# Row maxima of attention scores: from a PE transpose to a round trip through DRAM

## The chip, the cores and the metric

The kernel runs on one core of a Trainium2 chip. The metric is the device time of one execution in microseconds (us); lower is better. A core has five engines that run side by side, each working through its own instructions in order: PE (TensorE, matrix products; PEld are its weight loads), DVE (VectorE), ACT (ScalarE), POOL (GpSimd) and SP (SyncE), which here does nothing but issue DMA transfers. Engines wait for each other, and for transfers, through semaphores.

## The reference

The input x has 4 batches of 1024 tokens with 128 features. The block is half a mixture-of-experts FFN, attention, and half the same FFN again, each on a layer norm of x and added to x. The attention, cut to what matters here, with 16 heads of 64:

```python
scores = jnp.einsum('bhqd,bhkd->bhqk', q, k) * scale
attn = jax.nn.softmax(scores, axis=-1)
out = jnp.einsum('bhqk,bhkd->bhqd', attn, v)
out = out.transpose(0, 2, 1, 3).reshape(b, s, H * DH)
out = out @ w_out.T + residual
```

The softmax needs the largest score of each query row. The kernel computes it before the scores that it exponentiates.

## The kernel before

The three stages are FFN, attention and FFN. Attention takes most of the time, and the change lies in it.

**Units and slots.** Attention is cut into 64 units `U`: two heads (`hh` 0 and 1) of one batch by 512 queries. A unit has 8 slots, one for each 128 keys; two slots are a group `g`, so a unit is 4 groups. The loop over `g` (L908) writes each engine's instructions in the order in which Python emits them; nothing reorders them later. `self.at(g, fn)` puts `fn` into a list for the end of group `g`, and `run_later(g)` (L930) runs that list in the order of entry. So `at(self.group, ...)` means the end of the group being emitted, and `at(self.group + 1, ...)` the end of the next.

**Two passes.** `passA` runs 15 slots ahead (`AHEAD`). It computes a rough score tile of 128 queries by 512 keys for both heads into the PSUM tile `ps_a` (L675), and DVE reduces it to maxima (L676). After the eighth part of a unit, L679 folds the two halves of keys and negates: `m8` is 128 partitions (query within a block) by 8 columns (2 heads by 4 query blocks), and `max_row` is scheduled.

`score` computes the transposed scores, keys on partitions and queries along the free dimension, as four products added in PSUM (L703). The fourth multiplies a row of ones with `maxr[U % 2]`, whose rows 0 and 64 hold the negated maxima of the two heads for the unit's 512 queries; that subtracts each query's maximum. `maxr` therefore needs each maximum in a row, while `m8` has it in a column. ACT exponentiates (L707), `values` multiplies with the latents (L726).

**How the maxima become rows.** `max_row` transposes `m8` on PE against an identity into one of two spare banks of `ps_s` (L685), DVE copies the 8 x 128 result to `mr` (L687), and one group later two DMAs, one for each head, write 4 x 128 floats each into row 0 or 64 of `maxr` (L689).

**Denominators.** `den(U)` (L730) sums the exponentials on PE, ACT copies them to `dsb`, and then the sums make a trip through DRAM: `d<-dsb` and `dT<-d` (L745, L746) at the end of the next group, a reciprocal on DVE (L754), `d<-rT` and two `rB<-d` broadcasts (L757, L759) at the end of the group after that. DVE multiplies with `rB` two groups later (L766), and the output products (L771) follow. `dT<-d` reads what `d<-dsb` wrote, so SP waits for that transfer to land before it issues the next, and all that SP has behind it waits too.

**SP's list.** All DMAs are issued by SP, in order: loads of Q and K for the unit pair three ahead (`QT<-qs`, `KT<-ks`, four at a time), rotary-embedding results to DRAM (`qs` or `ks` `<-hi_r` and `<-eo`), latents fetched (`C_l<-cs`), the denominators' trip, and the maxima. Completion is counted on eight semaphores used in turn, so a DMA also waits for the one eight places before it where that is not known to be over.

Of the kernel before, what the change touches and what calls it, by code (L numbers as in the profile page):

```python
# [9 lines left out]
F32 = mybir.dt.float32  # L10
F32R = mybir.dt.float32r
# [26 lines left out]
class Kernel:  # L38
# [625 lines left out]
    def passA(self, a):  # L664

        nc = self.nc
        U, i = divmod(a, 8)
        P, half = divmod(U, 2)
        qb, kk = divmod(i, 2)
        if i == 0:  # L670
            self.m_of[U] = self.ms.tile([128, 2, 4, 2], F32, name="m")
        q0 = half * 512 + qb * 128
        for hh in range(2):
            r = slice(64 * hh, 64 * hh + 64)
            nc.tensor.matmul(self.psA[:, hh, :], self.QT[P % 3][r, 0, q0:q0 + 128], self.KT[P % 3][r, 0, kk * 512:kk * 512 + 512], start=True, stop=True)  # L675
        nc.vector.tensor_reduce(self.m_of[U][:, :, qb, kk], self.psA, AX.X, ALU.max)  # L676
        if i == 7:
            m = self.ms.tile([128, 8], F32R, name="m8")
            nc.vector.tensor_reduce(m, self.m_of.pop(U).rearrange("p h q k -> p (h q) k"), AX.X, ALU.max, negate=True)  # L679
            self.at(self.group + 1, lambda: self.max_row(U, m))  # L680

    def max_row(self, U, m):
        nc = self.nc
        pt = self.aux()
        nc.tensor.transpose(pt[0:8, 0:128], self.f(m), self.ident)  # L685
        mr = self.ms.tile([8, 128], F32R, name="mr")
        nc.vector.tensor_copy(mr, pt[0:8, 0:128])  # L687
        for hh in range(2):
            self.at(self.group + 1, lambda hh=hh: self.dma(out=self.maxr[U % 2][64 * hh:64 * hh + 1, :], in_=mr[4 * hh:4 * hh + 4, :]))  # L689

    def score(self, s, hh, k):

# [335 lines left out]
```

## Time and profile before

| What | Value |
|---|---|
| Median of 3 runs | 1803.73 us (1801.5 to 1804.94) |
| The profiled execution | 1803.11 us, of which its span is 1801.3 us |
| Busy: PE / PEld / DVE / ACT / POOL | 1726.3 / 1030.3 / 1339.9 / 908.9 / 1339.3 us |
| First FFN stage (0 to 260 us), PE busy | 218.7 us |
| Attention (260 to 1650 us), PE busy | 1372.5 us |
| Last FFN stage (1650 to 1801 us), PE busy | 135.2 us |
| Transposes L685 | 64, 0.27 us each |
| Copies to `mr`, L687 on DVE | 64, 0.27 us each |
| DMAs `maxr<-mr` | 128, 0.63 us of SP each, 2 KB each |
| From their issue to landing (semaphore events), median | 1.9 us |
| DMAs `dT<-d` / `d<-rT` (128 rows of 32 B) | 1.6 / 1.4 us from issue to landing, median |

The span runs from the first to the last instruction of the core. A row of the timeline gives the start in us from the beginning of the span, the length in us, engine, line of the kernel, operation, output and inputs by name, their shapes, and how many instructions were merged into the row; a bracket at its end gives the idle time before it and the instruction that ended that. An SP row is the time for issuing a DMA only; when its data has landed is seen in the semaphore events, and the bytes moved in the packet records.

### The profile page before, as it was taken

Reading aid. Unit: us, or ns where it says so; the run is one execution under the profiler, and the core shown is the slowest. Engines: PE = TensorE matmul, PEld = TensorE weight load, DVE = VectorE, ACT = ScalarE, POOL = GpSimd, SP = SyncE. Lnnn points to the kernel's source line nnn. Section 1 sums busy time; section 2 is a strip of 40 time slices with the busy share of each in tenths; the row PEclk is TensorE's granted clock in tenths of the full one; section 3 lists DMA queues with packets and bytes.
Section 4 is the critical chain, followed back from the end, with each engine's and each line's share of the span. In section 5 each row is a group of like instructions: output and inputs, shape, how many; then the busy total and the mean of one; then the engine's idle time right before and its main releaser. Section 6 shows DMA issues by size and latency. Waiting matters only on the chain.

```text
span 1801.3 us, 31304 instructions
## 1 busy us (share of the span) xinstructions
PE 1726.3 (96%) x11492; PEld 1030.3 (57%) x11492; DVE 1339.9 (74%) x1903; ACT 908.9 (50%) x1916; POOL 1339.3 (74%) x803
## 2 busy tenths in 40 slices
PE   7988889999999999999999999999999999999898
PEld 5777655555555555555555555555555555556676
DVE  6776658877777778777688777788777776835787
ACT  4666555444545445554444445454444444445454
POOL 4458678778887788877788777788888765556566
PEclk9999989999999999999999999999999999999899
DMA  6025445444444444454444544454444432124443
GB/s 196 1 71 170 135 129 165 145 145 147 130 142 142 150 145 130 130 153 142 141 135 136 160 140 131 143 142 147 136 144 140 130 95 72 31 96 129 129 124 100
DMA packets 129674, 232.80 MB, mean 129 GB/s; under 512 B 36336, under 2 KB 49776, under 8 KB 128880
## 3 DMA queue, kind: packets, MB, share of 16 engines
q1 hardware_dynamic: 129520, 230.80, 42.7%
q8 instruction: 90, 1.47, 0.4%
q14 instruction: 64, 0.52, 0.1%
HBM read 146.45 MB, written 84.02 MB: 128 GB/s over the span
## 4 chain that ended last, share of the span: by engine, by line
PE 78%; DVE 7%; ACT 7%; POOL 3%; issue 3%; DMA 1%; SPq 1%; ACTq 0%; POOLq 0%; DVEq 0%
PE psc L726 24%; PE ps_s L703 21%; PE ps_a L675 8%; PE ps_s L738 5%; ACT p L707 4%; PE psx L771 4%; PE ps_s L400 3%; PE ps_s L479 3%; PE psx L593 2%; DVE m L676 2%; PE psc L371 1%; PE psc L479 1%; PE psx L434 1%; PE ps_s L434 1%; ACT dtmp L383 1%
## 5 line engine op out<-in xcount | busy, mean ns | idle before, releaser
L676 DVE TENSOR_REDUCE m<-ps_a 128x2 f32<-128x1024 f32 x512 | 627.3, 1225 | 324.1 <-PE ps_a L675 323.9
L707 ACT ACTIVATE p<-ps_s 128x512 f32<-128x512 f32 x1024 | 531.0, 601 | 605.6 <-PE ps_s L703 605.4
L719 POOL TENSOR_TENSOR acc<-acc,p 128x1024 f32<-128x1024 f32 x256 | 609.7, 2382 | 43.0 <-ACT p L707 31.6
L726 PE MATMUL psc<-p,ckn 128*64 128x512 f32 x2048 | 496.2, 605 | 0.0
L703 PE MATMUL ps_s<-QT,KT 64*128 64x512 f32 x3072 | 447.3, 393 | 0.1
L719 POOL TENSOR_TENSOR acc<-p 128x1024 f32<-128x1024 f32 x64 | 152.2, 2377 | 251.4 <-ACT p L707 251.3
L703 PEld LDWEIGHTS ps_s<-QT,KT 64*128 64x128 f32 x3072 | 296.7, 185 | 60.2 <-issue 3.2
L726 PEld LDWEIGHTS psc<-p,ckn 128*64 128x64 f32 x2048 | 124.3, 136 | 213.7 <-issue 199.4
L675 PE MATMUL ps_a<-KT,QT 64*128 64x512 f32 x1024 | 234.6, 450 | 11.2 <-DVE m L676 11.0
L675 PEld LDWEIGHTS ps_a<-KT,QT 64*128 64x128 f32 x1024 | 98.5, 184 | 229.9 <-issue 83.8
L703 PE MATMUL ps_s<-maxr,one_row 64*128 64x512 f32 x1024 | 210.0, 392 | 1.0 <-DMA maxr<-mr 1.0
L612 POOL TENSOR_TENSOR eo<-eo,hi_r 128x512 fp32r<-128x512 f32 x128 | 185.0, 1463 | 0.0
L766 DVE TENSOR_TENSOR osb<-osb,rB 128x512 f32<-128x512 f32 x64 | 153.8, 2403 | 3.0 <-DMA rB<-d 3.0
L384 POOL TENSOR_TENSOR X<-X,dtmp 128x512 f32<-128x512 f32 x54 | 69.0, 1278 | 73.2 <-ACT dtmp L383 66.7
L703 PEld LDWEIGHTS ps_s<-maxr,one_row 64*128 64x128 f32 x1024 | 103.4, 185 | 23.0 <-DMA maxr<-mr 2.2
L487 POOL TENSOR_TENSOR p<-eo,p 128x512 fp32r<-128x512 f32 x42 | 62.6, 1496 | 42.0 <-ACT p L486 35.5
L602 POOL TENSOR_TENSOR eo<-rt,rt 128x512 f32<-128x512 f32 x64 | 81.8, 1279 | 0.0
L600 POOL TENSOR_TENSOR eo<-rt,rt 128x512 f32<-128x512 f32 x64 | 81.8, 1278 | 0.0
L607 ACT CAST hi_r<-eo 128x512 fp32r<-128x512 f32 x128 | 74.6, 640 | 6.9 <-DMA qs<-hi_r 3.6
L400 PE MATMUL ps_s<-xs,wg 128*128 128x512 f32 x192 | 66.6, 457 | 11.8 <-DVE p L408 10.7
L728 ACT COPY osb<-psc 128x512 f32<-128x512 f32 x64 | 37.6, 588 | 72.8 <-PE psc L726 72.8
L771 PEld LDWEIGHTS psx<-G,osb 128*128 128x128 f32 x496 | 60.8, 193 | 21.2 <-issue 21.2
(194 smaller groups left out, 2131.8 us busy)
## 6 DMA issues: line engine op xcount, KB each, us to landing
C_l<-cs SPq DMA_DIRECT2D x64, 512.0 KB
QT<-qs SPq DMA_DIRECT2D x256, 128.0 KB
KT<-ks SPq DMA_DIRECT2D x256, 128.0 KB
qs<-hi_r SPq DMA_DIRECT2D x32, 512.0 KB
qs<-eo SPq DMA_DIRECT2D x32, 512.0 KB
ks<-hi_r SPq DMA_DIRECT2D x32, 512.0 KB
ks<-eo SPq DMA_DIRECT2D x32, 512.0 KB
rB<-d SPq DMA_DIRECT2D x128, 128.0 KB
```

Source lines behind the costliest of these rows:

```text
L400: nc.tensor.matmul(p, w[:, a, e, :], xs[:, c, :], start=k == 0, stop=k == 2)
L600: nc.gpsimd.tensor_tensor(w["eo"][:, 0, :], w[0, 0], w[1, 1], ALU.subtract)
L612: nc.gpsimd.tensor_tensor(eo.bitcast(F32R), eo, self.f(w["hi"][:, int(stage[2]), :]), ALU.subtract)
L675: nc.tensor.matmul(self.psA[:, hh, :], self.QT[P % 3][r, 0, q0:q0 + 128], self.KT[P % 3][r, 0, kk * 512:kk * 512 + 512], start=True, stop= ...
L676: nc.vector.tensor_reduce(self.m_of[U][:, :, qb, kk], self.psA, AX.X, ALU.max)
L703: nc.tensor.matmul(ps, w, x, start=k == 0, stop=k == 3)
L707: nc.scalar.activation(self.p_of[s][:, hh, :], ps, AF.Exp, scale=0.125)
L719: nc.gpsimd.tensor_tensor(acc, self.p_of[s - 1] if c == 1 else acc, self.p_of[s], ALU.add)
L726: nc.tensor.matmul(self.psC[64 * hh:64 * hh + 64, :], self.ckn[b % 2][:, c, :], self.p_of[s][:, hh, :], start=c == 0, stop=c == 7)
L738: nc.tensor.matmul(pd[32 * n:32 * n + 32, 0:256], self.ones, part[:, n // 2, 256 * (n % 2):256 * (n % 2) + 256], start=k == 0, stop=k == D ...
L766: nc.vector.tensor_tensor(osb, osb, rB, ALU.mult)
L771: nc.tensor.matmul(po[:, i * 128:(i + 1) * 128], osb[:, i * 128:(i + 1) * 128], self.G[:, j, :], start=True, stop=True)
```

## The change

The transpose, the copy to `mr` and the two DMAs go. At the end of the group in which L679 runs (one group earlier than the transpose was) a DMA writes `m8` as it is to a DRAM tile `d3` of 128 x 8. At the end of the next group (one group earlier than the old DMAs) a single DMA fills rows 0 and 64 of `maxr` from there. Its source walks `d3` along columns: for each head `h` and query block `q` the 128 values `p`, which lie 8 floats apart. There are four such DRAM tiles, used in turn. The values that reach `maxr` are the same as before.

```diff
@@ -677,16 +677,13 @@
         if i == 7:
             m = self.ms.tile([128, 8], F32R, name="m8")
             nc.vector.tensor_reduce(m, self.m_of.pop(U).rearrange("p h q k -> p (h q) k"), AX.X, ALU.max, negate=True)
-            self.at(self.group + 1, lambda: self.max_row(U, m))
+            self.at(self.group, lambda: self.max_row(U, m))
 
     def max_row(self, U, m):
         nc = self.nc
-        pt = self.aux()
-        nc.tensor.transpose(pt[0:8, 0:128], self.f(m), self.ident)
-        mr = self.ms.tile([8, 128], F32R, name="mr")
-        nc.vector.tensor_copy(mr, pt[0:8, 0:128])
-        for hh in range(2):
-            self.at(self.group + 1, lambda hh=hh: self.dma(out=self.maxr[U % 2][64 * hh:64 * hh + 1, :], in_=mr[4 * hh:4 * hh + 4, :]))
+        d = self.dram.tile([128, 8], F32, name=f"d3_{U % 4}")
+        self.dma(out=d, in_=m)
+        self.at(self.group + 1, lambda: self.dma(out=self.maxr[U % 2][0:128:64, :].rearrange("h (q p) -> h q p", p=128), in_=d.rearrange("p (h q) -> h q p", h=2)))
```

## The prediction

> **What bounds the kernel now.** I read the stretches of the span first, then the chain of waits. The row below is the attention stage: length, then the busy time of PE, PEld, DVE, ACT and POOL.
>
> ```profile
> 260.00:1650.00 1390.00, 1372.46 (x9683) 750.00 (x9681) 1043.28 (x1306) 684.97 (x1373) 1087.43 (x584) 1.00 0.44 132
> ```
>
> ```profile
> PE 78%; DVE 7%; ACT 7%; POOL 3%; issue 3%; DMA 1%; SPq 1%; ACTq 0%; POOLq 0%; DVEq 0%
> ```
>
> PE is busy for 1372 of 1390 us at full clock (1.00), and 78% of the chain that ended last is PE. An instruction taken off PE here shortens the span by nearly its own pace; DMA matters only where its landing comes after the moment at which an engine of that chain wants the data. DVE (1043 us) has room on average, but works in order.
>
> Then I read the timeline of one cycle. A unit U (8 slots, 4 groups) takes 21 to 23 us; this is the end of one group and the next two.
>
> ```profile
> 910.00 2.25 SPq L47 DMA_DIRECT2D KT<-ks  x4
> ...
> 912.35 0.52 SPq L745 DMA_DIRECT2D d<-dsb  x1
> ...
> 913.78 0.39 PE L593 MATMUL psx<-C_l,wup 64*128 64x512 f32 x1
> 913.78 0.39 PE L593 MATMUL ps_s<-C_l,wup 64*128 64x512 f32 x1
> ...
> 914.11 0.27 PE L685 MATMUL ps_s<-ident,m 128*8 128x128 f32 x1
> ...
> 914.31 1.94 PE L726 MATMUL psc<-p,ckn 128*64 128x512 f32 x8
> ...
> 915.31 0.33 SPq L746 DMA_DIRECT2D dT<-d  x1
> ...
> 916.17 2.28 SPq L47 DMA_DIRECT2D QT<-qs  x4
> ...
> 920.55 0.20 DVE L754 RECIPROCAL rT<-dT 128x8 f32<-128x8 f32 x1
> ...
> 920.77 0.34 SPq L757 DMA_DIRECT2D d<-rT  x1
> 921.11 1.23 DVE L676 TENSOR_REDUCE m<-ps_a 128x2 f32<-128x1024 f32 x1 [0.37 <-PE ps_a L675]
> ...
> 922.37 1.15 SPq L759 DMA_DIRECT2D rB<-d  x2
> 922.76 0.40 PE L675 MATMUL ps_a<-KT,QT 64*128 64x512 f32 x2
> ...
> 923.61 1.35 SPq L47 DMA_DIRECT2D maxr<-mr  x2
> ```
>
> The transpose (L685) sits in PE's stream between the rope products and the values. The two maxr DMAs go out at 923.61, at the tail of SP's list, where nothing urgent follows. The denominators' round trip through DRAM (d<-dsb, dT<-d, reciprocal, d<-rT, rB<-d) runs through the middle of SP's list, and DVE's reciprocal stands in front of a reduce on which PE's next passA waits.
>
> **What goes: PE and DVE.** In the 55 cycles with rope products ahead, the first L726 matmul starts 0.13 us after the preceding matmul's end; without a transpose between, L726 starts 0.07 us before it (193 cases after den, outp and others). So a transpose costs 0.20 us of PE's pace: 55 x 0.20 = 11.2 us, and 8 late cycles (0.26 to 0.51 us gaps) give 3.0 more: 14 us. I count 0.85 of it, since the stage's PE is not on the chain in every cycle (DVE and ACT hold 14%): **12 us**. DVE loses 64 casts of 0.27 us, 17 us. DVE's reduces wait 324 us for PE in all, so I count nothing. PSUM bank ps_s is released earlier; its next writer comes after PE's 1.94 us of values anyway.
>
> **What goes: waits for maxr.** PE, weight loads included, waited 3.2 us for the old DMA. The new gather is issued near 912.3 in place of 923.6 for a use at 926.8 (the first maxr product of the unit), so these waits go. I count 1 us, as some of them stand behind a late reciprocal.
>
> **What is added on SP.** The old pair of DMAs takes 2 x 0.63 us of issuing per unit. The new write of the column block (128 rows of 32 B, like d<-rT: 0.33 us to issue, 1.4 us to land) needs the L679 reduce (906.79) and is issued near 907.0, when SP stands idle until 909.58 (ks<-hi_r). Nothing is delayed by it. The gather (nearest row d<-dsb, 0.52 us; few rows per DMA) takes its place a group later, after KT<-ks and **ahead of d<-dsb and dT<-d**: the listing of SP's instructions has KT x4, gather, d<-dsb, dT<-d, ks<-eo, QT x4, d<-rT. Its own wait, for the column block, is over some 4 us earlier. Behind it stand the denominators.
>
> **What the gather costs.** It moves 1024 single floats: 4 KB, 4 B each. The trace of before has no such DMA. Its semaphore events show that a DMA with 128 rows posts 16 of them and one with 4 rows (d<-dsb, maxr<-mr) only 5. The Trainium skill ("DMA: Bandwidth & Descriptors", in "Why a DMA increments its semaphore by 16 and not by 1") says that the engine count is the largest up to 16 that divides the outermost dimension of both sides, and, under "Rules for kernel authors", that a strided last dimension becomes one descriptor per element. Both speak against this change: outermost is 2, so 512 descriptors fall on each of 2 engines. Spread as the 128-row rows are, it would be 64 each.
>
> The price of a descriptor from the packet records: in lnsb<-in_ln_sb (128 pieces of 8 B from DRAM) the eight packets of one engine start 5.9 ns apart, and so do the 32 B packets of dT<-d. A packet of 4 to 32 B is recorded as 7 to 9 ns long. With 256 B (wv, 1024 packets) starts of one engine are about 14 ns apart. So 512 descriptors take 3.0 us at 5.9 ns, 4.6 us at 9 ns, 7.2 us at 14 ns. A floor is the 16-engine reading: 64 x 5.9 ns = 0.4 us. Generating 1024 descriptor pairs is not slower: those 1024 packets all started within 1.6 us. I take **3.0 us**, the pace of the rows nearest in size, though those bursts are 8 long and not 512. The same page's fit of a DMA's time ("Anatomy of one DMA": 2.0 us plus bytes over 436 GB/s, for another issuing path) would make it 2.0 us like any 4 KB transfer, delaying nothing; it has no term for descriptors, so the packet rows decide.
>
> **What is late next.** d<-dsb has 4 rows, so by the same rule it uses engines that the gather fills. The median KT transfer takes 4.1 us to land, so both queue behind KT, and d<-dsb lands later by about the gather's 3.0 us. SP waits for that before dT<-d: 915.3 becomes 918.4. The cover is the time from the landing of dT to the reciprocal. By the semaphore events it is about 3.7 us in the units where KT loads precede (every second one, 32), and 5.3 to 6.5 us in the others. PE's gain takes 0.2 us of it. After it come 0.37 us in which DVE was idle before L676, and 0.42 us between the end of that reduce (922.34) and the passA at 922.76. So a gather costs nothing up to 3.5 + 0.8 = **4.3 us**, or 8.4 ns a descriptor, in one half, and up to about 6.8 us in the other; each us beyond is paid by PE, 32 times per half. At 3.0 us the cover holds. A few units have less (2.3 to 3.1 us before the 0.8): 1 us in all. The held-up ks<-eo and QT loads issue 3 us later and then push d<-rT by 0.7 us; the time from rB's landing to its use is 4.5 us at the median, and QT pieces are used some five groups later. The gather lands near 918, used at 926.8: covered up to about 12 us.
>
> **Sum.** 1803.1 (profiled execution: span 1801.3 and 1.8 around it; 0.6 below the median of 1803.7) - 12 - 1 + 1 = **1791 us**.
>
> **Rivals.**
> - *Descriptors at 9 to 14 ns* (for: their recorded length, 9 ns; 512 in a row may not sustain a burst's pace; against: measured starts at 5.9). At 12 ns the gather is 6.1 us: 1.8 us past the cover in 32 units, +58 us against -12: **1849 us**. This is the case on the other side: the reciprocal waits for dT, DVE's reduce stands behind it, PE stands for passA. It decides from 9.1 ns (4.65 us), where 32 x 0.37 us eat the 12.
> - *Descriptors bound by latency*, over 14 ns (for: no long run of tiny reads is in the trace; against: 256 B packets already flow at 14). At 7.2 us: 2.9 x 32 + 0.4 x 32 = 106, so **1897 us**; at 23 ns (11.8 us) both halves pay, 240 + 160, near 2190.
> - *The transpose's time was not on the path* (for: DVE's and ACT's 14% of the chain; against: PE at 98.7% of this stage): gather hidden, PE's gain lost in waits on the exponentials, **1803 us**.
>
> **How the numbers follow.** Forecast 48%, its own range 1786 to 1798 (all 14 us and the 3 us of waits gained; or half the gain and cover missing in some units). Slower descriptors 27%, latency-bound 20%, no effect 5%. A change within 0.2% (3.6 us) can't be told from none. Faster by more: nearly all of the forecast, 47%; within: the no-effect case and 9 ns, 9%; slower 44%. The range runs from 1786 to 1895 and leaves out the latency case.
>
> **What would show it.** Right: L726 follows L593 at -0.07 us; the gather shows as 1024 packets of 4 B over about 3 us; dT<-d issues 3 us later after d<-dsb; DVE's reciprocal shows no wait for dT. Wrong: a row in which the reciprocal waits for dT<-d in half or all of the units, and PE's passA then waits for DVE's m; or a wait for maxr on PE.

## The result, and the profile after

The changed kernel takes a median of 1787.79 us (1782.91 to 1791.76, 6 runs) against 1804.54 us (1801.5 to 1805.81, 6 runs) for the kernel before: a ratio of 0.9905, 95% interval 0.9887 to 0.9923, or 14 to 20 us less. The forecast was 1791 us. Run again at the end of the study (run r1) it took 1781.15 us against 1806.01, ratio 0.9868 (0.9853 to 0.9884), 21 to 27 us less, which is below the forecast's own range of 1786 to 1798 us. The sign is certain; by the ratios the size differs by 7 us between two sessions of the same two kernels, and a good part of that goes with the granted clock (see "What stays open").

The first view is the attention stage by windows, columns as in the prediction (length, busy time of PE, PEld, DVE, ACT, POOL, granted clock, share and rate of the DMA engines), of the kernel after.

```profile
260.00:1650.00 1390.00, 1374.49 (x9697) 752.95 (x9694) 1041.16 (x1261) 691.43 (x1386) 1095.34 (x589) 1.00 0.48 134
```

Next the chain of waits on the page of the kernel after.

```profile
PE 78%; DVE 7%; ACT 7%; DMA 2%; POOL 2%; issue 2%; SPq 1%; ACTq 0%; DVEq 0%; POOLq 0%
```

PE still bounds the stage: busy for 1374 of 1390 us, 78% of the chain. A bound that has not moved gives back what was taken off it. Only DMA has grown, from 1% to 2%, and the busy share of the DMA engines from 0.44 to 0.48.

Where the time went is seen when the execution is cut at the starts of four matmuls: the first of all, the first and the last product with `maxr`, and the last of all.

| Profiled execution | From the first matmul to the first product with `maxr` | To the last product with `maxr` | To the last matmul |
|---|---|---|---|
| before | 237.5 us | 1386.8 us | 166.6 us |
| after | 242.3 us | 1372.2 us | 165.6 us |
| after, run r1 | 236.1 us | 1365.7 us | 165.6 us |

The gain is in attention, 14.6 and 21.1 us. In the first profile of the changed kernel 4.8 us were lost in the first FFN stage, at a mean granted clock of 0.93 in 0 to 260 us against 0.96 in the profile before; in r1 (0.96) they are not there. So that loss is not the change's.

The timeline of the cycle that the prediction read, in the kernel after (start in us, length in us, engine, line, operation):

```profile
910.47 2.27 SPq L47 DMA_DIRECT2D KT<-ks  x4
...
912.85 0.56 SPq L47 DMA_DIRECT2D maxr<-d  x1
...
913.51 3.89 SPq L742 DMA_DIRECT2D d<-dsb  x1
...
914.25 0.39 PE L593 MATMUL ps_s<-C_l,wup 64*128 64x512 f32 x1
...
914.58 1.94 PE L723 MATMUL psc<-p,ckn 128*64 128x512 f32 x8
...
919.03 0.34 SPq L743 DMA_DIRECT2D dT<-d  x1
...
920.81 0.19 DVE L751 RECIPROCAL rT<-dT 128x8 f32<-128x8 f32 x1
...
921.37 1.23 DVE L676 TENSOR_REDUCE m<-ps_a 128x2 f32<-128x1024 f32 x1 [0.36 <-PE ps_a L675]
```

Between the last rope product (ends at 914.64) and the first product of the values (914.58) nothing stands any more: the values start 0.06 us before the other's end, where they started 0.13 us after it. On SP the gather goes out between KT and `d<-dsb`, as listed. `dT<-d` follows `d<-dsb` 5.52 us after the latter's start, where before it took 2.96 (912.35 to 915.31). The reciprocal starts 1.78 us after `dT<-d` was issued, against 5.24 before: of the cover that hid the gather, hardly anything is left.

The tile view of the DRAM tiles `d` in the kernel after (count, then minimum, median and maximum of SP's time for issuing one, in ns) shows something that the prediction did not have.

```profile
L47 SPq DMA_DIRECT2D d<-m x64: 320/338/783, 215.3 to 1588.8; - x64
...
L742 SPq DMA_DIRECT2D d<-dsb x64: 523/3465/4338, 279.5 to 1626.2; - x64
```

Issuing `d<-dsb`, right behind the gather, holds SP for 3.47 us, where it was 0.52 before. So SP itself stands while the gather's descriptors drain, and not only the data of `d<-dsb` come later. The column write `d<-m` is cheap to issue, as predicted (0.34 us). The waits of SP's queue in the kernel after (total us, times, longest) show that it is not cheap to wait for:

```profile
SPq L47 <- DMA d<-m: 82.5, 33, 8.3
```

That is every second unit, and the timeline of SP shows why:

```profile
883.44 0.61 SPq L47 DMA_DIRECT2D C_l<-cs  x1
884.09 2.26 SPq L47 DMA_DIRECT2D KT<-ks  x4
886.45 0.37 SPq L47 DMA_DIRECT2D d<-m  x1
889.42 0.38 SPq L47 DMA_DIRECT2D qs<-hi_r  x1
893.70 0.56 SPq L47 DMA_DIRECT2D maxr<-d  x1
894.36 3.45 SPq L742 DMA_DIRECT2D d<-dsb  x1
```

There the column write is issued behind a load of latents and four KT loads, 1 MB in all. By the semaphore events it lands 4.3 us or more after its issue in three quarters of these units (at most 7.2), and the gather goes out 0.1 us after that.

What is left of the cover is read from the waits of the kernel after. These are the reciprocal's waits for `dT<-d`, first of the kernel before, then of the kernel after:

```profile
DVE rT L754 <- DMA dT<-d: 10.7, 2, 6.6
...
DVE rT L751 <- DMA dT<-d: 23.1, 12, 15.1
```

One place, near the end of attention, makes 15.1 of the 23.1 us; the other eleven make 8.0 us. No wait for `maxr` is left on PE.

Of the waits of PE and its weight loads before, the longest that names something which the change removes is that of passA's weight loads for DVE's copy (first line: us in all, times, longest). After, they wait nearly as long for a rope instruction of DVE (second line):

```profile
PEld ps_a L675 <- DVE mr L687: 47.1, 58, 0.8
...
PEld ps_a L675 <- DVE rt L581: 40.6, 50, 0.8
```

What such a wait is worth is tested by e1b, which brings the copy back. The page's line on DMA packets of the kernel after shows the gathers by their number; before, 36,336 packets were under 512 B.

```profile
DMA packets 203528, 233.05 MB, mean 130 GB/s; under 512 B 110704, under 2 KB 123632, under 8 KB 202736
```

64 gathers of 1024 floats are 65,536 of the 74,368 that were added, and 64 column writes of 128 rows another 8,192.

### The profile page after: what moved, and what is told of

It is laid out like the page before. It is cut to its first block, busy times and chain, and to the rows that moved or that the text cites. A ratio compares the mean times of both kernels' runs of the same rounds, so it can differ in the third digit from the quotient of the medians.

```text
span 1790.0 us, 30996 instructions
## 1 busy us (share of the span) xinstructions
PE 1716.9 (96%) x11428; PEld 1025.4 (57%) x11428; DVE 1323.8 (74%) x1839; ACT 907.5 (51%) x1916; POOL 1338.6 (75%) x803
## 4 chain that ended last, share of the span: by engine, by line
PE 78%; DVE 7%; ACT 7%; DMA 2%; POOL 2%; issue 2%; SPq 1%; ACTq 0%; DVEq 0%; POOLq 0%
PE psc L723 25%; PE ps_s L700 21%; PE ps_a L675 8%; PE ps_s L735 5%; ACT p L704 4%; PE psx L768 4%; PE ps_s L400 3%; PE ps_s L479 3%; PE psx L593 2%; DVE m L676 2%; PE psc L371 1%; DMA d<-dsb 1%; PE psc L479 1%; PE psx L434 1%; PE ps_s L434 1%
## 5 line engine op out<-in xcount | busy, mean ns | idle before, releaser
L675 PE MATMUL ps_a<-KT,QT 64*128 64x512 f32 x1024 | 234.1, 451 | 9.5 <-DVE m L676 9.2
L675 PEld LDWEIGHTS ps_a<-KT,QT 64*128 64x128 f32 x1024 | 97.2, 184 | 230.9 <-issue 86.2
L700 PE MATMUL ps_s<-maxr,one_row 64*128 64x512 f32 x1024 | 206.4, 391 | 0.0
L700 PEld LDWEIGHTS ps_s<-maxr,one_row 64*128 64x128 f32 x1024 | 100.2, 184 | 21.1
L735 PE MATMUL ps_s<-p,ones 128*32 128x256 f32 x1024 | 68.5, 385 | 4.7 <-ACT p L704 0.9
```

Of the source, the lines that this page charges most:

```text
L700: nc.tensor.matmul(ps, w, x, start=k == 0, stop=k == 3)
L735: nc.tensor.matmul(pd[32 * n:32 * n + 32, 0:256], self.ones, part[:, n // 2, 256 * (n % 2):256 * (n % 2) + 256], start=k == 0, stop=k == D ...
```

## The experiments

Three theories stood at the start. **The prediction's:** the transposes' pace on PE is the gain, all else is covered. **Order:** the maxima only come earlier, and the gain is from waits for `maxr`. **Collision:** the gather costs a good part in front of the denominators, so that a better place would give more. Kernels of one session share runs of the kernel before: e1, e1b, e2b and e3 (1802.99 us); e4, e5 and e6 (1805.72); e3c, e9 and e10 (1801.9); r1 and r2 (1806.01). Ratios are against those.

**e1 and e1b: the transposes back, the new DMAs kept.** The transpose stands where it was and nothing reads it; e1b also has DVE's copy.

The edit of e1, in `max_row` behind the gather:

```diff
+        def dead():
+            nc.tensor.transpose(self.aux()[0:8, 0:128], self.f(m), self.ident)
+
+        self.at(self.group + 1, dead)
```

And what e1b has beyond it:

```diff
         def dead():
-            nc.tensor.transpose(self.aux()[0:8, 0:128], self.f(m), self.ident)
+            pt = self.aux()
+            nc.tensor.transpose(pt[0:8, 0:128], self.f(m), self.ident)
+            mr = self.ms.tile([8, 128], F32R, name="mr")
+            nc.vector.tensor_copy(mr, pt[0:8, 0:128])
```

> The changed kernel with the 64 transposes back in their old place on PE, their result read by nobody; the maxima still come through DRAM. If the gain is PE's pace (0.20 us a transpose at 55 places, 0.26 to 0.58 at 8), the time rises by 11 to 14 us over the changed kernel, to about 1800 us. If the gain came from DVE's copy or from the earlier DMA instead, it rises by less than 4 us, to at most 1792 us.

> As the run with the transposes back, and DVE's copy of 8 x 128 to SBUF back as well, again read by nobody. If DVE's 64 copies (0.27 us each) lie in idle time, the same time as with the transposes alone, within 3 us. If DVE counts, up to 17 us more, near 1815 us; then the DRAM trip itself would have cost something that DVE's relief paid for.

Measured: e1 1807.97 us, ratio 1.0035 (1.0016 to 1.0054); e1b 1806.93 us, 1.0031 (1.0018 to 1.0044). The gain is gone with the transposes: "not on the path" falls. The copy costs nothing, as the two agree within about 1 us, though in e1b passA's weight loads wait 47.1 us for it again. Both are slower than the kernel before, by 5.0 and 3.9 us between the medians. A part of that goes with the granted clock, whose median is 0.9875 and 0.987 in these runs and 0.9895 in the session's runs of the kernel before. Over all 55 runs of the kernel before in the experiments a straight line gives 1.4 us more for each thousandth of clock less; e1 lies 3.6 and e1b 2.6 us above that line. So beside the transposes the trip through DRAM seems to cost some 3 us, by this estimate.

**e2b: no transposes, no trip through DRAM either.** The kernel before without transposes and copies; the two old DMAs stay in their place and bring a constant. The row maxima are left out of the computation: -300 is added to every score in their place. All other work is done.

```diff
+        self.mr0 = const.tile([8, 128], F32R, name="mr0")
+        nc.gpsimd.memset(self.f(self.mr0), -300.0)
...
-        pt = self.aux()
-        nc.tensor.transpose(pt[0:8, 0:128], self.f(m), self.ident)
-        mr = self.ms.tile([8, 128], F32R, name="mr")
-        nc.vector.tensor_copy(mr, pt[0:8, 0:128])
+        mr = self.mr0
```

> The kernel before without transposes and copies; its two DMAs per unit write a constant tile (-300) into the rows, at their old place, so the row maxima are left out of the result. It has PE's gain and no gather. If the gather of the changed kernel is covered, as predicted, this is as fast as the changed kernel or up to 4 us slower (it keeps the old late DMAs): 1788 to 1792 us. If the gather has an uncovered price of 10 us or more, this one is faster by that: 1778 us or less.

Measured: 1787.82 us, ratio 0.9918 (0.9904 to 0.9932): 14.8 us less than before, with no gather and no column write at all. The changed kernel, at 0.9905 and 0.9868, is not slower than that; so in it the trip through DRAM costs nothing that shows, as far as sessions can be compared. Against the line through the runs before, e2b is 16.6 us faster and the changed kernel 15.6 and 19.1. e2b and e1b, on one chip, differ by 11.3 thousandths, 20 us: the transposes, and what the trip costs beside them.

**e3: the kernel before, with its transpose and DMAs one group earlier.**

```diff
-            self.at(self.group + 1, lambda: self.max_row(U, m))
+            self.at(self.group, lambda: self.max_row(U, m))
```

> The kernel before with max_row one group earlier, nothing else: transposes, copies and both DMAs stay, and the DMAs land one group sooner. If the waits for maxr (3.2 us in all) are all that the order brings, 1 to 4 us are gained: 1801 to 1804 us. If most of the gain came from the order, it would be near 1790 us.

Measured: 1839.95 us, ratio 1.0208 (1.0193 to 1.0223), 37 us slower. This tested something else than meant. The matmul records put +37.4 us between passA and the sums of the denominators, 0.6 us in each of the 61 places in which the transpose now stands, and the waits on PE and on the weight loads are at the same place:

```profile
PE ps_s L738 <- ACT p L707: 20.7, 62, 1.4
...
PEld ps_s L738 <- ACT p L707: 33.1, 63, 1.6
```

Before, that wait for ACT (PE and weight loads together) was 31.5 us, now 53.8. One group earlier the transpose shares its group, and the spare banks of `ps_s`, with the denominators; that this sharing is the cause was not isolated. What the order of the DMAs alone gives was left open.

**e3c: the kernel before, with only the two `maxr` DMAs earlier,** behind `dT<-d` of the same group.

```diff
+        self.soon = []
...
-            self.at(self.group + 1, lambda hh=hh: self.dma(out=self.maxr[U % 2][64 * hh:64 * hh + 1, :], in_=mr[4 * hh:4 * hh + 4, :]))
+            self.soon.append(lambda hh=hh: self.dma(out=self.maxr[U % 2][64 * hh:64 * hh + 1, :], in_=mr[4 * hh:4 * hh + 4, :]))
...
         for fn in self.later.pop(g, []):
             fn()
+        for fn in self.soon:
+            fn()
+        self.soon = []
```

> The kernel before with transposes and copies where they were, and only its two maxr DMAs moved one group forward, behind dT<-d. This prices the order alone, without the change of a PSUM bank that the earlier attempt brought with it. By the prediction's 3.2 us of waits, 1 to 4 us are gained: 1800 to 1803 us. If the late maxima cost more than the waits that name them, up to 9 us (what the gather behind dT<-d has over the kernel without transposes): 1795 us.

Measured: 1803.78 us, ratio 1.0000 (0.9990 to 1.0010, 14 runs). The time between the landing of `maxr` and its use rises from 1.8 to 9.2 us at the median, and the time does not move. "Order" falls.

**e4: scatter on the write, contiguous gather.** The same 1024 single floats, on the other side of the trip.

```diff
-        d = self.dram.tile([128, 8], F32, name=f"d3_{U % 4}")
-        self.dma(out=d, in_=m)
-        self.at(self.group + 1, lambda: self.dma(out=self.maxr[U % 2][0:128:64, :].rearrange("h (q p) -> h q p", p=128), in_=d.rearrange("p (h q) -> h q p", h=2)))
+        d = self.dram.tile([8, 128], F32, name=f"d3_{U % 4}")
+        self.dma(out=d.rearrange("c p -> p c"), in_=m)
+        self.at(self.group + 1, lambda: self.dma(out=self.maxr[U % 2][0:128:64, :], in_=d.rearrange("(h q) p -> h (q p)", h=2)))
```

> The changed kernel with the reordering moved to the write: the column block goes to DRAM as 8 x 128 (128 partitions outermost, 1024 single floats, 64 descriptors on each of 16 engines by my reading), and the gather reads two rows of 2 KB. If only the number of descriptors on one engine makes the gather long, the write takes about 64 x 5.9 ns = 0.4 us, d<-dsb issues and lands as before the change, and the slack ahead of the reciprocal comes back to 3 us and more. If the covered gather costs nothing, the time stays within 3 us of the changed kernel (1785 to 1791 us); if its remaining waits (23 us of DVE for dT<-d, mostly once) are on the path, it falls to 1775 to 1783 us. If single floats written to DRAM are dear, the write shows it, with waits for d<-m or maxr.

Measured: 2012.02 us, ratio 1.1143 (1.1116 to 1.1169). The expectation was missed by over 200 us. The timeline of SP in this kernel, in the cycle with the same loads:

```profile
907.88 0.38 SPq L47 DMA_DIRECT2D d<-m  x1
910.50 0.38 SPq L47 DMA_DIRECT2D ks<-hi_r  x1
910.94 3.25 SPq L47 DMA_DIRECT2D KT<-ks  x4
918.66 0.53 SPq L47 DMA_DIRECT2D maxr<-d  x1
919.28 0.55 SPq L742 DMA_DIRECT2D d<-dsb  x1
```

Its waits on SP's queue:

```profile
SPq L47 <- DMA d<-m: 448.3, 58, 15.0
```

In four writes whose packet records were read, the packets start within 2.0 to 5.5 us of the issue, but over all 64 the completion comes at 11.7 us at the median (9.1 to 15.3). SP stands until then, and the denominators stand behind it: the reciprocal waited 200.2 us for `dT<-d`, 61 times. The granted clock fell with it, to 0.95 over the run, so the 206 us are not waits alone. Behind the contiguous gather `d<-dsb` issues in 0.55 us again.

**e5: the gather twice.** A second column write and a second gather, into a tile that nobody reads, double the disputed cost.

```diff
+        self.spare = const.tile([128, 512], F32R, name="spare")
...
+        d2 = self.dram.tile([128, 8], F32, name=f"d4_{U % 4}")
+        self.dma(out=d2, in_=m)
+        self.at(self.group + 1, lambda: self.dma(out=self.spare[0:128:64, :].rearrange("h (q p) -> h q p", p=128), in_=d2.rearrange("p (h q) -> h q p", h=2)))
```

> The changed kernel with a second column write and a second gather of the same form into a tile that nobody reads, ahead of d<-dsb. The descriptors then take 6 us in a row. With the slack seen in the changed kernel (about 0.5 us in every second unit, 1 to 2 in the others, and 0.8 us between DVE and PE), 3 us more overrun it in all units: about 1.7 us x 32 + 0.7 us x 32, so 60 to 100 us slower than the changed kernel, 1850 to 1890 us. By the prediction's own cover (4.3 and 6.8 us) only every second unit pays, 1.7 us x 32: about 1840 us. If engines are never held up by the gather, the time stays below 1795 us.

Measured: 1956.91 us, ratio 1.0826 (1.0793 to 1.0859): 168 to 175 us above the changed kernel (151 over the kernel before, plus the 17 to 24 gained), where 60 to 100 was expected. In the tile view SP is held twice:

```profile
L47 SPq DMA_DIRECT2D spare<-d x64: 3193/3592/4217, 215.3 to 1749.5; - x64
L746 SPq DMA_DIRECT2D d<-dsb x64: 523/3287/3497, 276.8 to 1777.5; - x64
```

and the wait has arrived at DVE in nearly all units, not in half of them:

```profile
DVE rT L755 <- DMA dT<-d: 165.0, 58, 18.3
```

Per unit the whole loss is 2.6 to 2.7 us, where the second gather makes `dT` land 3.2 us later after the first gather's issue (10.57 us at the median against 7.39 in r1). Not all of that is waiting, though. In the records the granted clock is either 1.00 or 0.50, and attention spends 92 us at 0.50 in e5 against 0.2 us in r1. At most half of such time is lost, so the waits themselves cost at least 1.9 us a unit (163 us more than r1 in attention, less 46, over 63 intervals). So of the cover 0.5 to 1.3 us was left. Whether the clock fell because PE waited isn't shown; the one came with the other. This is the prediction's rival on the other side, brought about.

**e6: the gather behind `dT<-d`.** It is kept back until `den` has entered its DMAs, and goes out behind them in the same group.

```diff
+        self.gather = None
...
-        self.at(self.group + 1, lambda: self.dma(out=self.maxr[U % 2][0:128:64, :].rearrange("h (q p) -> h q p", p=128), in_=d.rearrange("p (h q) -> h q p", h=2)))
+        gather = lambda: self.dma(out=self.maxr[U % 2][0:128:64, :].rearrange("h (q p) -> h q p", p=128), in_=d.rearrange("p (h q) -> h q p", h=2))
+        if U < 2:
+            self.at(self.group + 1, gather)
+        else:
+            self.gather = gather
...
         self.at(self.group + 1, turn)
+        gather, self.gather = self.gather, None
+        if gather:
+            self.at(self.group + 1, gather)
```

> The changed kernel with the gather issued behind dT<-d instead of ahead of d<-dsb. If the cost of a gather is only what queues behind it on SP and on two DMA engines, d<-dsb issues in 0.5 us again, the slack ahead of the reciprocal is back at 3 us and more, and the gather holds up the rotary write and the Q and K loads behind it instead, which have time. Time within 3 us of the changed kernel if the gather was covered; 3 to 10 us less if not. If the first unit's use of maxr comes too soon, PE waits for maxr and the time rises.

Measured: 1780.23 us, ratio 0.9866 (0.9847 to 0.9885). On SP's timeline of e6 the denominators pass, and the DMA that is held is now `ks<-eo`:

```profile
903.86 0.56 SPq L747 DMA_DIRECT2D d<-dsb  x1
906.83 0.33 SPq L748 DMA_DIRECT2D dT<-d  x1
907.25 0.57 SPq L47 DMA_DIRECT2D maxr<-d  x1
907.91 3.17 SPq L47 DMA_DIRECT2D ks<-eo  x1
```

The slack ahead of the reciprocal is back at 4.6 and 3.6 us (medians of the two kinds of unit). Taken alone, 0.9866 against 0.9905 looks like 7 us gained by the place. But the two ratios come from two sessions.

**r1 and r2: the changed kernel and e6 again, side by side.**

> The changed kernel itself, unaltered, beside the next one on one chip, so that the two can be compared without another chip's times between them. About 0.990 of the kernel before.

> The gather behind dT<-d once more, on the same chip as the changed kernel. If its place ahead of d<-dsb has a real price, 5 to 9 us below the changed kernel here too (0.986 of before); if the first measurement of it only fell on a chip or a moment that suited it, within 3 us.

Measured: r1 (the changed kernel) 1781.15 us, 0.9868 (0.9853 to 0.9884); r2 (e6) 1780.52 us, 0.9868 (0.985 to 0.9887). The same to within about 4 us, and at the same granted clocks (0.987, 0.991 and twice 0.992 in each). The 7 us were between the sessions, and "collision" falls too: in its place ahead of the denominators the gather costs nothing that shows.

**e9 and e10: sixteen bytes a descriptor.** passA takes every fourth query, so that column `q` of `m8` holds queries 4p+q and the gather's source has four neighbouring floats: 128 descriptors an engine. e10 has the gather behind `dT<-d` as well, by the edit of e6. The edit of e9:

```diff
-            nc.tensor.matmul(self.psA[:, hh, :], self.QT[P % 3][r, 0, q0:q0 + 128], self.KT[P % 3][r, 0, kk * 512:kk * 512 + 512], start=True, stop=True)
+            nc.tensor.matmul(self.psA[:, hh, :], self.QT[P % 3][r, 0, half * 512 + qb:half * 512 + 512:4], self.KT[P % 3][r, 0, kk * 512:kk * 512 + 512], start=True, stop=True)
...
-        self.at(self.group + 1, lambda: self.dma(out=self.maxr[U % 2][0:128:64, :].rearrange("h (q p) -> h q p", p=128), in_=d.rearrange("p (h q) -> h q p", h=2)))
+        self.at(self.group + 1, lambda: self.dma(out=self.maxr[U % 2][0:128:64, :].rearrange("h (p q) -> h p q", q=4), in_=d.rearrange("p (h q) -> h p q", h=2)))
```

> The changed kernel, in its own order, with the queries of a unit dealt to the four query blocks in turn (block q holds queries 4p + q), so that a row of maxima is made of 16-byte pieces: 128 descriptors on each of two engines instead of 512. If the gather's cost to the changed kernel is its length in front of d<-dsb, the gather takes about 128 x 6 to 8 ns = 0.8 to 1 us, d<-dsb is hardly held up on SP, the slack ahead of the reciprocal is back above 2.5 us, and the time comes near that of the gather behind dT<-d: about 1780 us. If the order on SP is what matters and not the length, it stays near 1788 us. If weight loads with a stride of 4 are slower on PE, it rises.

> Both: 16-byte pieces and the gather behind dT<-d. If nothing of the gather's cost is left once it stands behind dT<-d, the same as that kernel, 1778 to 1782 us. If its 3 us still delay ks<-eo, the Q and K loads and d<-rT enough to be waited for, 2 to 5 us less: 1775 us.

Measured: e9 1819.43 us, 1.0087 (1.0070 to 1.0105); e10 1817.38 us, 1.0083 (1.0068 to 1.0098). The DMA side did what it should: the gather lands in 3.07 us against 5.35 at the median, `d<-dsb` issues in 1.45 us against 3.47, and the slack is 5.4 and 3.3 us. The time was lost on PE, at the weight loads of passA. The lines of L675 in e9 (count, then minimum, median and maximum in ns):

```profile
L675 PEld LDWEIGHTS ps_a<-KT,QT x1024: 304/306/329, 179.6 to 1609.7; 64*128 64x128 f32 x171
```

and in the kernel after:

```profile
L675 PEld LDWEIGHTS ps_a<-KT,QT x1024: 182/183/285, 184.8 to 1586.8; 64*128 64x128 f32 x171
```

A stride of four floats makes the load 0.12 us longer; the matmul records have 30 us more between passA and the scores. That is the length of these loads: 0.12 us in each of 249 places. In e10 the slack is 6.5 and 4.0 us, and the time is the same as in e9: more room in front of the denominators gives nothing, as in r1 and r2.

## Why the prediction was right

The matmul records give an account by kinds of neighbours on PE: the time from the start of one matmul to the start of the next, summed over the kernel. The places that changed most:

| Pair on PE | Change, first profile after | Change, r1 |
|---|---|---|
| rope product, transpose, values (55 places) | -11.3 us | -11.2 us |
| passA, transpose, values | -2.4 us | -2.4 us |
| passA, transpose, FFN product | -2.35 us | -2.3 us |
| one product with `maxr` to the next | -2.9 us | -2.9 us |
| product with `maxr` to passA | -2.2 us | -3.8 us |

These are the places picked for their size; the others moved by up to 2.3 us, some of them up. All places together make -10.7 us in the first profile, with its loss in the FFN stage, and -23.3 us in r1.

- **Pace of a transpose, 0.20 us:** right. 55 places predicted at 11.2 us gave 11.3 and 11.2. The late cycles, 3.0 predicted, gave 2.4. The values start 0.06 us before the end of the rope product in the timeline (-0.07 predicted).
- **The factor of 0.85:** this term of the sum was mis-sized. It made 12 of 14. 13.6 came, plus 2.3 for the first transposes, beside an FFN product, which the prediction did not count; e2b, without transposes or trip, gained 14.8 by itself. By these sums nothing had to be taken off for the 14% of the chain that is DVE and ACT.
- **DVE's copy at nothing:** right (e1 against e1b).
- **Waits for `maxr`, 1 us of 3.2:** the 3.2 us on the page are gone. Of the 2.9 us between products with `maxr` (table) 1.8 fall in the first group of the units, where `maxr` is used first. But e3c takes the waits for `maxr` away alone, with the transposes left, and gains 0 (-2 to +2 us). So no run shows that these waits gave anything by themselves.
- **Column write:** 0.34 us to issue: right. "Over some 4 us earlier": in one half of the units it is over before the gather goes out, by 2.2 us at the median and not 4; wrong in the other, where it queues behind 1 MB of loads and holds the gather up. That half had been given the longer cover, 5.3 to 6.5 us (slack before, by the semaphore events, 6.24 us at the median); it is down to 0.97 (r1: 0.54). That this half still held is luck: SP's wait for the column write, 2.5 us each time, was in no sum.
- **Gather, 5.9 ns a descriptor on two engines, 3.0 us:** right. The packet records of one gather have 1024 packets of 4 B at 85 in 250 ns over two engines, 5.9 ns each on an engine, 3.0 us in all. So 512 in a row keep the pace of bursts of eight. Both rules of the Trainium skill ("DMA: Bandwidth & Descriptors", "Why a DMA increments its semaphore by 16 and not by 1" and "Rules for kernel authors") that the prediction weighed hold in this trace: two engines, and one descriptor for each element. The gather posts three semaphore events, one more than its engines, as the 4-row DMAs post five. The descriptors are as many and as badly spread as the rules say; they cost no time because the drain lies beside other work.
- **`dT<-d` 3 us later:** 2.6 us here by the two timelines, but half by another way than predicted: SP's own issue of `d<-dsb` is held.
- **Cover:** the cost was right (1 us; r1 against r2: 0, give or take 4), the margin only in one half. In the units with KT loads right ahead of the gather 3.5 less 3.0 us should be left ahead of the reciprocal, and 0.39 us is (r1: 0.45). In the others some 3 us should be left, and 0.97 is (r1: 0.54). How much of the 0.8 us of cushion behind the reciprocal exists is not settled: e5 leaves 0.5 to 1.3 us for slack and cushion together. That is 1.0 to 2.5 ns a descriptor above the 5.9 measured, so the cover ends at 6.9 to 8.4 ns, and in all units at once. The prediction had it end at 8.4 ns in one half and far later in the other, so its rival on the other side was nearer than it said.

Rivals: descriptors at 9 to 14 ns, and bound by latency, did not come (5.9 ns). That the transpose's time is not on the path is refuted by e1 and e2b, which put it back and take it out.

**What stays open.** Beside the transposes the trip through DRAM costs some 3 us by the estimate above (e1, e1b), without them nothing that shows (the changed kernel against e2b, in different sessions). In e1 and e1b the matmul records have it between the product with `maxr` and passA in the last group of a unit, 27 to 29 us over the kernel against 24.9 before and 20 to 22 after. No run isolates why.

The gain is 17 us between the medians of the first session and 25 in r1, and a good part of the difference goes with the granted clock. The changed kernel's profile has 48 us at a clock of 0.50 in the first session and 27 us in r1; at most half of that time is lost, so this makes up to 10 of the 12.7 us between the two profiled executions. Runs at a clock of 0.991 say the same: the changed kernel took 1784.1 us in the first session and 1781.4 in r1, the kernel before 1799.6 and 1801.7 in the experiments. At like clock the change is worth 15 to 20 us. Why the clock was lower in the first session, and what the last 3 us are, stays open.

## What to carry to other kernels

Small work on the engine that is busy for 99% of a stage is worth its full pace, and a transfer of a thousand tiny descriptors may replace it where its drain is hidden; but cost that transfer on the issuing queue as well, with the DMA behind it held as long as the drain lasts, and with every transfer queued ahead of the data that it waits for. Read what is left of a cover after a change, and not only that it held: here 0.4 to 1.0 us of some 4 to 6 was left at the median, and a version with the gather behind the urgent pair (e6) has 3.6 us and more in the same time. Put two versions into one session, and their granted clocks beside their times, before their difference is believed: between sessions the same ratio moved by 0.4%. And a long wait on a page may be worth nothing: the 47 us for DVE's copy were.

## What the runs showed of the hardware that was not expected

- A DMA issued behind one with 512 descriptors on an engine held SP for 3.2 to 3.5 us at the median, whether it has 4 rows (`d<-dsb`, 0.52 before) or is a large store (`ks<-eo` in e6, 0.37 before); behind 128 descriptors an engine 1.45 us (e9). The added 2.9 and 0.9 us are about what the descriptors take at 5.9 to 6.8 ns each.
- Single floats scattered to DRAM are another matter than gathered from it: the packets start within 2.0 to 5.5 us, complete only at 9.1 to 15.3 us after issue (e4), where the gather lands at 4.75 to 5.98 us.
- The 4 KB column write lands 5.0 us after its issue at the median in the half of the units where 1 MB of loads is ahead of it, 3.0 us in the other half; the shortest takes 1.4 us.
- A weight load of 64 x 128 floats with a stride of four floats takes 306 ns, contiguous 183 ns (e9 and the kernel after).
- Where the denominators came late, the granted clock was lower too: attention spends 92 us at 0.50 in e5 and 163 us in e4, against 5 us in the kernel before and 0 to 7 us in the changed one.
